# The residual x as transposes at the head of the output projection's accumulation group, in place of identity products at its end

## The chip, the cores and the metric

The kernel runs on one core of one Trainium2 chip. The metric is the device time of one execution, in microseconds (us). The kernel before was timed in three runs, and the median counts. Beside them stands one profiled execution, from which all durations and starts of single instructions come; it is its own execution, with its own time.

## What is computed

The input x has 256 channels and 48 x 48 positions, that is 2304 tokens of 256 numbers, all in float32. Two layers follow each other. Cut to what matters, with `gn` a normalization over groups of channels and `ln` one over each token:

```
# layer 0
xt  = tokens of gn(x)                       # 2304 x 256
q, k, v = xt @ Wq.T + bq, xt @ Wk.T + bk, xt @ Wv.T + bv
A   = softmax(q @ k.T / 8)                  # every token's 4 heads are rows of their own: 9216 x 9216, head size 64
t   = x.T + (A @ v) @ Wo.T + bo             # the residual x is added, as tokens
# layer 1
t   = t + slice_attention(ln(t))            # 64 soft slices, attention among them, back to tokens
t   = t + moe(ln(t))                        # 8 experts, each token in its two best
out = t.T as 256 x 48 x 48
```

The change lies in the line that makes t in layer 0. The kernel holds x with its channels on the partitions, while t has its tokens on the partitions, so x has to be turned where it is added.

## The kernel before, in words

The work has stages, one after the other: projections of q, k and v (to about 69 us of the profiled execution's span), attention (to about 1244 us), the slice attention of layer 1, the routing of tokens to experts, the experts, and a last transposition of the output.

Attention takes the 9216 queries in 18 blocks of 512 (`NQB`), and for every block all 9216 keys in 36 pairs of 128-key tiles (`NPAIR`). For a pair, `scores` (line 507) makes four score products on TensorE (PE) into PSUM tile `s`, and ScalarE (ACT) takes their exponential into `p`. `sums` adds `p` into `acc` on VectorE (DVE), and `times_values` (line 539) makes the four value products into PSUM tile `av`. The value products of a pair come on PE after the score products of the next. All these products use a 64 x 64 part of PE's array each. A float32 product is two passes on PE, and each pass leaves its own record in the profile with its own weight load (PEld). So a pair has eight records of `s` and eight of `av`.

After a block comes `close` (line 552), in which DVE makes `both` from `acc` and `up` from `av`. Then comes `between` (line 584), called at the second pair of the next block. It calls `follow` (line 572), which puts up to four steps of a side pipeline on PE, each for another 128-token tile:

- `out_proj` (line 373) for tile k-2: the attention output `OT` of that tile times `WoT`, with two channel halves c that add up, and then the tile's columns of `x_sb` times the identity matrix `ident`, one product for each 128 channels, each into its own half of the 256 columns. All of it is one accumulation group in the first 256 columns of PSUM tile `pa`. In each of these calls the first operand is the stationary one, whose load is the weight load; in the profile's names the moving operand comes first (`pa<-ident,x_sb`).
- `turn` (line 407) for the tile before that: two transposes of the normalized tile `tn`, into the other columns of `pa`.
- `slices` (line 417): the slice logits, into `pb`.
- `gather` (line 453): sums of tokens by slice, into `pb`.

`between` then adds the softmax sums `pb<-both,ones` to PE's stream. What these steps need of DVE and ACT (in `out_proj`: `add`, which reads `pa` and adds the bias `bo_bc` into `t_sb`, then `spread` and `norm`) is put into a list in the order of a rank written beside each step, and one entry is taken from that list at each of the following pairs.

`out_proj` is called for tiles 0 to 15 inside attention and for tiles 16 and 17 after it, in the loop at line 666, where the PSUM tile is called `pm`. There all of the last block's outputs have to be finished first.

The order on every engine is written out by hand: `pe`, `dve`, `act` and `pool` are wrapped in `InOrder` (line 49), which keeps instructions in program order. Line 57, where the wrapper issues, therefore stands for most instructions in the profile, and one goes by the tiles' names. Semaphore waits are put in by the tile framework from the tiles' uses.

Of the kernel before, what the change touches and what calls it, by code (L numbers as in the profile page):

```python
# [15 lines left out]
P = 128  # L16
# [46 lines left out]
def layers(  # L63
# [14 lines left out]
    pe, dve, act, pool = (InOrder(tc, e) for e in (nc.tensor, nc.vector, nc.scalar, nc.gpsimd))  # L78
# [73 lines left out]
    x_sb = l0.tile([P, 2, NT], FP, name="x_sb")  # L152
# [77 lines left out]
    with proj, tc.tile_pool(name="ps_pj", bufs=5, space=PSUM) as ps_pj, tc.tile_pool(  # L230
# [80 lines left out]
        for i in range(NTT):  # L311
            pv = ps_pj.tile([P, 512], FP, name="pp", tag="pp")
            for c in range(2):
                nc.tensor.matmul(  # L314
                    pv[:, 0:C], xn[:, c, i * P : (i + 1) * P], WvT[:, c, :],
                    start=(c == 0), stop=(c == 1),
# [11 lines left out]
        for ci in range(2):  # L328
            cols = slice(ci * P, (ci + 1) * P)
            for k in range(2):  # L330
                nc.tensor.matmul(
                    pw[:, ci * S : (ci + 1) * S], W0T[:, k, cols], Ws_sb[:, k, :],
                    start=(k == 0), stop=(k == 1),
                )
            for k in range(2):
                nc.tensor.matmul(
                    pw[:, 192 + ci * E : 192 + (ci + 1) * E], WoutT[:, k, cols], Wg_sb[:, k, :],
                    start=(k == 0), stop=(k == 1),
# [34 lines left out]
    def out_proj(i, ps):  # L373

        tok = slice(i * P, (i + 1) * P)
        g, u = divmod(i, TG // P)
        for c in range(2):
            pe.matmul(
                ps[:, 0:C], OT[:, g % 2, c, u * P : (u + 1) * P], WoT[:, c, :],
                start=(c == 0), stop=False,  # L380
            )
        for c in range(2):
            pe.matmul(
                ps[:, c * P : (c + 1) * P], x_sb[:, c, tok], ident, start=False, stop=(c == 1)
            )

        def add():
            dve.tensor_tensor(t_sb[:, i, 0:C], ps[:, 0:C], bo_bc, ALU.add)

        def spread():  # L390
            s6 = small.tile([P, 6], FP, name="s6", tag="s6")
            dve.bn_stats(s6, t_sb[:, i, 0:C])
            dve.bn_aggr(stats[:, i, :], s6)
            ve = small.tile([P, 1], FP, name="ve", tag="ve")
            dve.tensor_scalar(ve, stats[:, i, 1:2], 1e-5, None, ALU.add)
            pool.tensor_tensor(rstd_t[:, i : i + 1], ve, mhalf[:, 0:1], ALU.pow)
            return ve

        def norm():
            dve.tensor_scalar(  # L400
                tn[:, i % 6, :], t_sb[:, i, 0:C], stats[:, i, 0:1], rstd_t[:, i : i + 1],
                ALU.subtract, ALU.mult,
            )

        return [(2, add), (3, spread), (7, norm)]
# [67 lines left out]
    def attention():  # L473


        with tc.tile_pool(name="pexp", bufs=5) as pexp, tc.tile_pool(
# [95 lines left out]
            def follow(k):  # L572

                pa = ps_side.tile([P, 512], FP, name="pa", tag="pa")
                pb = ps_side.tile([P, 512], FP, name="pb", tag="pb")
                work = []
                for lag, (step, ps) in enumerate(
                    ((out_proj, pa), (turn, pa), (slices, pb), (gather, pb))
                ):
                    if 0 <= k - 2 - lag < NTT - 2:  # L580
                        work.extend(step(k - 2 - lag, ps))
                return work, pb
# [83 lines left out]
    for k, step in enumerate((out_proj, turn, slices)):  # L666
        work = []
        for i in range(NTT - 2, NTT):
            work.extend(step(i, ps_o.tile([P, 512], FP, name="pm", tag="pm")))
        if k == 0:  # L670
            weights_transposed(0, 4)
            weights_transposed(4, 4)
        if k == 2:
            pe.matmul(den, ones, sw_sum, start=True, stop=False)
        for w in in_turn(work):
            w()
    for c in range(2):
        for i in range(NTT - 2, NTT):
            pe.matmul(
                pts[:, c * S : (c + 1) * S], tn[:, i % 6, c * P : (c + 1) * P], sw[:, i, :],  # L680
                start=(i == NTT - 2), stop=(i == NTT - 1),
# [19 lines left out]
    with tc.tile_pool(name="sa", bufs=1) as sa:  # L701
        tw = sa.tile([P, C + E], FP, name="tw")
        with sums_done, tc.tile_pool(name="ps_b", bufs=4, space=PSUM) as ps_b, tc.tile_pool(
# [4 lines left out]
            for m in range(2):  # L708
                for c in range(2):
                    pe.matmul(  # L710
                        ph[:, m, :], W0_sb[:, c, m * P : (m + 1) * P], ts_sum[:, c * S : (c + 1) * S],
                        start=(c == 0), stop=(c == 1),
# [23 lines left out]
            for u in range(2):  # L736
                ph = ps_b.tile([P, 2, S], FP, name="ph", tag="mm")
                phs.append(ph)
                for kind in range(2):
                    j = 2 * kind + u  # L740
                    for c in range(2):
                        pe.matmul(
                            ph[:, kind, :], Wqkv_sb[:, c, j * P : (j + 1) * P], hsT[:, c, :],
                            start=(c == 0), stop=(c == 1),
# [62 lines left out]
            for w in range(2):  # L807
                pe.matmul(
                    pw, tokT[:, w].rearrange("p a s -> p (a s)"), Wout_sb[:, w, :],
                    start=(w == 0), stop=(w == 1),  # L810
# [407 lines left out]
```

## Time and profile before

| What | Value |
|---|---|
| Median of three timed runs | 1645.1 us (1644.57 to 1647.49) |
| Profiled execution's own time | 1642.84 us |
| Span of the profiled execution, first to last instruction | 1641.1 us |
| Mean granted PE clock | 0.973 of full |
| PE busy, 69 to 1238 us (attention) | 1167.46 of 1169.00 us |
| DVE and ACT busy there | 899.75 and 683.15 us |
| `pa<-WoT,OT`, 128x256, records in attention | 64, mean 405 ns |
| `pa<-ident,x_sb`, 128x128, records in attention | 64, mean 274 ns |
| `pm<-ident,x_sb`, 128x128, records after attention | 8, mean 375 ns |

How to read it: a PE record lasts from the start of a pass to its result's arrival, and the next pass starts long before that. So records overlap, and the sum of their durations is more than the time that they take from PE. The time that a pass takes is the distance from its start to the next one's. In a timeline, the first number is the start in us from the span's start, the second how long the whole group of records lasted, and brackets hold the idle time of that engine before it with what ended it.

### The profile page before, as it was taken

What the parts mean: (1) busy time and instruction counts of PE and PEld (TensorE: products, weight loads), DVE (VectorE), ACT (ScalarE), POOL (GpSimd) and SP (SyncE); (2) the same over time, 40 slices, a digit from 0 to 9 for tenths busy, and PEclk for the clock granted to TensorE, in tenths of its full rate; (3) what the DMA queues carried; (4) which work ended last, traced back from release to release, by engine and by line L of the source; (5) the groups of instructions that cost most, each with busy time, mean ns of one, the idle gap of its engine ahead of it and who ended that gap; (6) DMA issues with size and microseconds to landing.
All of it is one profiled execution on the core that took longest, in us unless ns stands there. A gap on an engine that the chain in (4) does not pass through costs nothing.

```text
span 1641.1 us, 31749 instructions
## 1 busy us (share of the span) xinstructions
PE 1574.2 (96%) x13178; PEld 793.9 (48%) x13178; DVE 1046.9 (64%) x1361; ACT 811.1 (49%) x1100; POOL 149.7 (9%) x129
## 2 busy tenths in 40 slices
PE   7999999999999999999999999999997589999995
PEld 3633343333333333333333333333344389999994
DVE  6577777687787786877777878878785721111111
ACT  2355555565555655656556556556552313333321
POOL 0000000000000000000000000000000253333321
PEclk9999999999999999999999999999997679999998
DMA  4000000000000000000000000000005456666665
GB/s 135 1 1 1 1 1 1 1 1 1 2 1 1 2 1 2 1 1 1 1 1 1 1 1 1 1 1 1 1 2 185 161 174 186 172 188 183 176 164 169
DMA packets 39878, 79.26 MB, mean 48 GB/s; under 512 B 3581, under 2 KB 26186, under 8 KB 39594
## 3 DMA queue, kind: packets, MB, share of 16 engines
q1 hardware_dynamic: 32042, 66.35, 12.1%
q0 software_dynamic: 7680, 10.75, 3.7%
q8 instruction: 108, 1.77, 0.5%
q14 instruction: 48, 0.39, 0.1%
HBM read 64.64 MB, written 12.45 MB: 47 GB/s over the span
## 4 chain that ended last, share of the span: by engine, by line
PE 93%; DVE 3%; DMA 3%; ACT 0%; issue 0%; POOL 0%; SPq 0%; ACTq 0%; POOLq 0%; DVEq 0%
PE s L57 34%; PE av L57 34%; PE ph L57 8%; PE py L57 8%; PE pa L57 2%; DMA t_d<-y,slot_t 2%; PE pb L57 1%; PE pw L57 1%; PE pp L285 1%; PE pp L289 1%; PE pp L314 1%; PE pt L57 1%; DVE s L57 0%; DMA Wq_raw<-in_L_conv_Wq_dram 0%; PE pm L57 0%; ACT p L57 0%
## 5 line engine op out<-in xcount | busy, mean ns | idle before, releaser
L57 DVE TENSOR_TENSOR acc<-acc,p 128x1024 f32<-128x1024 f32 x612 | 748.1, 1222 | 256.7 <-ACT p L57 248.8
L57 ACT ACTIVATE p<-s 128x1024 f32<-128x1024 f32 x648 | 663.3, 1024 | 492.9 <-PE s L57 482.8
L57 PE MATMUL av<-p,v_sb 64*64 64x512 f32 x5184 | 675.8, 590 | 1.4 <-ACT p L57 0.7
L57 PE MATMUL s<-q,kk 64*64 64x512 f32 x5184 | 674.9, 589 | 0.0
L57 PEld LDWEIGHTS s<-q,kk 64*64 64x64 f32 x5184 | 202.0, 133 | 351.2 <-issue 180.9
L57 PEld LDWEIGHTS av<-p,v_sb 64*64 64x64 f32 x5184 | 195.8, 131 | 358.1 <-ACT p L57 202.3
L57 ACT ACTIVATE hid<-ph,bcol 128x128 f32<-128x128 f32 x312 | 89.4, 368 | 221.3 <-PE ph L57 220.6
L57 PEld LDWEIGHTS ph<-xT,w 128*128 128x128 f32 x1248 | 147.7, 195 | 2.8 <-DVE xT L57 0.9
L57 PE MATMUL ph<-xT,w 128*128 128x128 f32 x1248 | 148.1, 278 | 0.5 <-DVE xT L57 0.5
L57 PE MATMUL py<-w_sb,hid 128*128 x624 | 147.1, 379 | 0.0
L57 POOL TENSOR_TENSOR rstd_t<-ve,mhalf 128x1 f32<-128x1 f32 (+1 forms) x21 | 27.5, 1312 | 1252.1 <-DVE ve L57 1252.1
L57 DVE COPY xT<-pt 128x256 f32<-128x256 f32 x40 | 17.0, 425 | 172.6 <-PE pt L57 172.6
L57 PEld LDWEIGHTS py<-w_sb,hid 128*128 128x128 f32 x624 | 112.8, 190 | 12.2
L1086 POOL DMA_INDIRECT t_d<-y,slot_t x39 | 61.7, 1583 | 98.7 <-DVE y L57 88.4
L57 DVE TENSOR_TENSOR y<-py,b_bc 128x256 f32<-128x256 f32 x39 | 16.6, 425 | 68.6 <-PE py L57 68.6
L1026 POOL DMA_INDIRECT xs<-tn_d,slot_t x36 | 38.3, 1064 | 93.0 <-PE pt L57 83.9
L57 DVE RECIPROCAL rinv<-pb 128x256 f32<-128x256 f32 x18 | 31.5, 1750 | 0.0
L57 DVE TENSOR_TENSOR acc<-p 128x1024 f32<-128x1024 f32 x18 | 22.1, 1225 | 8.4 <-ACT p L57 8.4
L302 DVE TENSOR_SCALAR q<-pp,bcol 64x512 f32<-64x512 f32 (+1 forms) x30 | 20.8, 694 | 9.4 <-PE pp L285 9.1
L57 PE MATMUL pw<-what,t_sb 128*128 128x86 f32 x72 | 15.7, 422 | 6.7 <-POOL what L57 6.7
L57 DVE TENSOR_REDUCE up<-av 128x512 f32<-128x1024 f32 x18 | 21.9, 1216 | 0.0
L285 PE MATMUL pp<-t_sb,WqT 128*128 128x512 f32 (+1 forms) x40 | 19.0, 601 | 0.3 <-DVE t_sb L276 0.3
(251 smaller groups left out, 607.5 us busy)
## 6 DMA issues: line engine op xcount, KB each, us to landing
w<-in_L_ffn_W_dram SPq DMA_DIRECT2D x40, 1024.0 KB, 5.3
w_sb<-in_L_ffn_W_dram SPq DMA_DIRECT2D x8, 1024.0 KB, 10.6
x_sb<-in_x_dram SPq DMA_DIRECT2D x4, 576.0 KB
t_d<-t_sb SPq DMA_DIRECT2D x3, 768.0 KB, 3.9
tn_d<-tn SPq DMA_DIRECT2D x3, 768.0 KB, 3.7
tt<-t_d SPq DMA_DIRECT2D x4, 512.0 KB
out_dram<-ob SPq DMA_DIRECT2D x4, 512.0 KB, 3.5
b_bc<-in_L_ffn_b_dram SPq DMA_DIRECT2D x1, 1024.0 KB
```

What stands on the lines that cost most here:

```text
L57: return self.tc.keep_in_program_order(getattr(self.engine, name)(*args, **kwargs))
L285: nc.tensor.matmul(pq[:, 0:tn], WqT[:, c, cols], xn[:, c, toks], start=(c == 0), stop=(c == 1))
L289: nc.tensor.matmul(pk[:, 0:tn], WkT[:, c, cols], xn[:, c, toks], start=(c == 0), stop=(c == 1))
L302: nc.vector.tensor_scalar(dst, pq[rows, 0:tn], bcol[rows, B_Q + m : B_Q + m + 1], 0.125, ALU.add, ALU.mult,)
L314: nc.tensor.matmul(pv[:, 0:C], xn[:, c, i * P : (i + 1) * P], WvT[:, c, :], start=(c == 0), stop=(c == 1),)
L1026: nc.gpsimd.indirect_dma_start(out=xs, out_offset=None, in_=tn_d[:, :], in_offset=bass.IndirectOffsetOnAxis(ap=slot_t[:, s : s + 1], axis= ...
L1086: nc.gpsimd.indirect_dma_start(out=t_d[:, :], out_offset=bass.IndirectOffsetOnAxis(ap=slot_t[:, s : s + 1], axis=0), in_=y, in_offset=None ...
```

## The change

In `out_proj`, x comes first. Its two products become transposes (the flag `is_transpose`, with the same operands), the first of which opens the accumulation group. The two projection products follow, add onto what the transposes wrote, and close the group. Nothing else is edited; the function serves both places that call it.

```diff
         g, u = divmod(i, TG // P)
+
+        for c in range(2):
+            pe.matmul(
+                ps[:, c * P : (c + 1) * P], x_sb[:, c, tok], ident, start=(c == 0), stop=False,
+                is_transpose=True,
+            )
         for c in range(2):
             pe.matmul(
                 ps[:, 0:C], OT[:, g % 2, c, u * P : (u + 1) * P], WoT[:, c, :],
-                start=(c == 0), stop=False,
-            )
-        for c in range(2):
-            pe.matmul(
-                ps[:, c * P : (c + 1) * P], x_sb[:, c, tok], ident, start=False, stop=(c == 1)
+                start=False, stop=(c == 1),
             )
```

More of the change, by code (lines that the diff above doesn't have):

```diff
@@ L378, in out_proj @@
             pe.matmul(
-                ps[:, 0:C], OT[:, g % 2, c, u * P : (u + 1) * P], WoT[:, c, :],
-                start=(c == 0), stop=False,
+                ps[:, c * P : (c + 1) * P], x_sb[:, c, tok], ident, start=(c == 0), stop=False,
+                is_transpose=True,
             )
@@ L383, in out_proj @@
             pe.matmul(
-                ps[:, c * P : (c + 1) * P], x_sb[:, c, tok], ident, start=False, stop=(c == 1)
+                ps[:, 0:C], OT[:, g % 2, c, u * P : (u + 1) * P], WoT[:, c, :],
+                start=False, stop=(c == 1),
             )
```

## Prediction

> **What bounds the kernel now.** I read the page first: busy shares, then the chain that ended last.
>
> ```profile
> PE 1574.2 (96%) x13178; PEld 793.9 (48%) x13178; DVE 1046.9 (64%) x1361; ACT 811.1 (49%) x1100; POOL 149.7 (9%) x129
> ...
> PE 93%; DVE 3%; DMA 3%; ACT 0%; issue 0%; POOL 0%; SPq 0%; ACTq 0%; POOLq 0%; DVEq 0%
> ```
>
> TensorE (PE) holds 93% of the chain, so a piece taken from its stream shortens the span unless something else arrives late in its place. Next the groups of tile pa, the PSUM bank in which `out_proj` works.
>
> ```profile
> L57 PE MATMUL pa<-WoT,OT x64: 379/379/483, 259.2 to 1197.5; 128*128 128x256 f32 x64
> ...
> L57 PE MATMUL pa<-ident,x_sb x64: 272/275/275, 260.1 to 1198.0; 128*128 128x128 f32 x64
> ...
> L57 PE MATMUL pa<-ident,tn x32: 272/273/328, 324.6 to 1213.3; 128*128 128x128 f32 x32
> ```
>
> Attention treats 16 tiles, so the 32 identity products of x left 64 records, two passes each; the 32 transposes of tn, same shape and type, left 32, one pass each. The durations (275 and 273 ns) are alike and say nothing of the price, because records overlap. The price is the distance between starts, and the timeline of PE has it. Here is one boundary between query blocks, with ScalarE (ACT) and VectorE (DVE) just after it:
>
> ```profile
> 712.76 1.13 PE L57 MATMUL pa<-WoT,OT 128*128 128x256 f32 x4
> 713.08 0.81 PE L57 MATMUL pa<-WoT,OT 128*128 128x256 f32 x3
> 713.73 0.61 PE L57 MATMUL pa<-ident,x_sb 128*128 128x128 f32 x4
> 714.17 0.38 PE L57 MATMUL pa<-ident,tn 128*128 128x128 f32 x2
> 714.39 0.56 PE L57 MATMUL pb<-Wl,tnT 128*128 128x72 f32 x4
> ...
> 717.98 1.02 ACT L57 ACTIVATE p<-s 128x1024 f32<-128x1024 f32 x1 [3.42 <-PE s L57]
> 719.04 1.23 DVE L57 TENSOR_TENSOR acc<-acc,p 128x1024 f32<-128x1024 f32 x1 [3.86 <-ACT p L57]
> ```
>
> (The second line is the same group from its second pass on.) Second to fourth projection pass: 0.65 us, 0.216 each. Four x passes: 0.44, 0.11 each. Two tn transposes: 0.22, again 0.11 each. The first projection pass takes 0.32, since its weight load lies open. At the block's other end ACT and DVE stand idle for 3.42 and 3.86 us, waiting for PE.
>
> The last block has one place where one-pass transposes come first after attention's narrow products, and the end of attention has tiles 16 and 17:
>
> ```profile
> 1213.16 0.44 PE L57 MATMUL pa<-ident,tn 128*128 128x128 f32 x2
> 1213.44 0.23 PE L57 MATMUL pb<-Wl,tnT 128*128 128x72 f32 x1
> ...
> 1244.71 2.05 PE L57 MATMUL pm<-WoT,OT 128*128 128x256 f32 x4 [4.33 <-DVE ends_of L57]
> 1246.55 1.06 PE L57 MATMUL pm<-ident,x_sb 128*128 128x128 f32 x4
> 1247.40 1.91 PE L57 MATMUL pm<-WoT,OT 128*128 128x256 f32 x4
> 1247.65 0.42 DVE L57 TENSOR_TENSOR t_sb<-pm,bo_bc 128x256 f32<-128x256 f32 x1 [3.08 <-PE pm L57]
> 1249.11 0.78 PE L57 MATMUL pm<-ident,x_sb 128*128 128x128 f32 x4
> 1249.93 0.42 DVE L57 TENSOR_TENSOR t_sb<-pm,bo_bc 128x256 f32<-128x256 f32 x1 [1.85 <-PE pm L57]
> ```
>
> Two transposes at the head take 0.28, open load included. At the end PE starts cold after a wait of 4.33 us for DVE (mean granted clock 0.57 from 1242 to 1250 us), so passes take twice as long: 1.71 for four of projection, 0.85 for four of x. The second add on DVE, at 1249.93, starts all that follows.
>
> **What the Trainium skill says.** "Perfetto Trace Analysis", section Transposes, advises the transpose mode for logical transposes, since it skips the arithmetic. The trace agrees in passes: 32 records against 64. "TensorE: Matmul & The Clock Gate", Part 4, gives about 275 ns for a transpose inside a kernel. The record agrees (273), but the pitch that matters here is 110. The same page, Part 2, LDWEIGHTS, prices a load by its columns, 128/1.2 = 107 ns; that fits 110, so a one-pass transpose is load-bound and no cheaper than one x pass. "PSUM — Partial Sum Buffer", The four PSUM rules, says that an fp32 transpose sets the written bits and that a later product without the opening flag adds onto them. It gives no cost, and no line of this trace shows a product adding onto a transpose.
>
> **The change part by part.**
>
> *Passes removed.* Each tile's x goes from four passes to two.
>
> *Order.* Transposes now open the group and projection closes it. Old stage, 712.76 to 714.17: 1.41 us. New stage: 0.28 for two transposes at the head (from 1213.16 to 1213.44) plus 4 x 0.216 = 0.86 of projection, whose loads hide under the pass before: 1.14. That is 0.27 less per tile: two passes, 0.22, and 0.05 from an open load under which the second transpose's own load begins sooner. Low end 0.22, if the 0.05 isn't had. 16 x 0.27 = 4.3 us, low end 3.5.
>
> *Waits.* The built instruction order shows the wait on DVE for the free bank moved from the first projection pass to the first transpose; attention's next products and the softmax sums `pb<-both` are queued behind it, but it was met long before, since the records show no idle PE there. The sums also need both, which DVE has at 258.86 in the tightest block, 1.80 before they start at 260.66. The next block's `av` needs DVE's up: in that block up ends at 259.99 and `av` starts at 261.24, a cover of 1.25 of which 0.27 goes. If it were gone, `av` would wait and the gain with it.
>
> *What is late next.* DVE works without a gap for some 13 us after 719, which could take a gain back. But that stretch begins after 3.86 us idle, released by ACT, and ACT by PE, so it moves forward with PE. DVE's add of this tile comes 12 us later (726.41); who reads PSUM doesn't matter. No DMA, SP or POOL instruction is moved.
>
> *Tiles 16 and 17.* Their first transpose carries the same waits on DVE and PE in the built order, so it can't use the 4.33 us. From PE's start to the second add: now 5.22. After, at the cold clock: 0.54 for two transposes at the head (the 0.28 about doubled), 1.71, 0.43 (half of 0.85), 1.71, and 0.25 until the add (1247.40 to 1247.65): 4.64. Saved 0.6; between 0.4 and 0.9, as the clock comes back earlier or later. The path goes on through this add, so it passes on whole.
>
> *After a transpose.* The unseen step is projection adding onto a fresh transpose. From below: nothing, as passes of x that add onto projection follow at 0.11. From above: PE waits for the transpose to drain, 0.273 in place of 0.11, so 0.16 a tile, 2.9 in 18. A gain is excluded, since the pass's load and stream remain. I take nothing.
>
> *Sum.* 4.3 + 0.6 = 4.9 us. On the profiled execution: span 1641.1 to 1636.2, its time 1642.84 to 1637.9. That execution lies 2.3 below the median of the three timed runs, so I take the saving from the median: 1645.1 - 4.9 = 1640.2. Ends without a stall: 3.5 + 0.4 and 4.4 + 0.9, so 1641.2 to 1639.8.
>
> **Rivals.**
>
> 1. *A drain after each transpose pair.* 18 x 0.16 = 2.9 given back: 1643.1, within 0.2%. For it: it is the one step that the trace lacks. Against: tn transposes are followed by other products at 0.11, and x's second pass adds onto its first at the same pitch.
>
> 2. *Slower: the clock.* Part 4 of the TensorE page says that transposes don't count as PE work for the clock. If two more of them at each boundary emptied one activity window (the page's Part 1: about 3.4 us), half a clock there would cost an estimated 1.7 us. In each of 16 boundaries that is 27: 1645.1 - 4.9 + 27 = 1667. It cancels the gain from three such windows on, and makes the kernel slower by over 0.2% from five. Against: tn's transposes are there already, and the granted clock is 1.00 over 21 to 1242 us.
>
> 3. *Not one pass.* If x still took two passes, only the reordering's 0.05 a tile would stay: 0.9 in 18, 1644.2. The tn records speak against it.
>
> 4. *Clock draws after attention.* The clock's mean is 0.62 from 1250 to 1331 us, and the three runs spread over 2.9 us. A draw 1.7 worse leaves 3.2 of the gain: 1641.9.
>
> **How the numbers follow.** Forecast 0.72; rival 1, 0.08; rival 2, 0.04; rival 3, 0.03; rival 4, 0.13. 0.2% is 3.3 us, about what a measurement of this kernel can tell from no change. The forecast lies 1.6 beyond it, inside the runs' spread: I give 0.66 of its chance and 0.08 of rival 4's to faster, and what is left, with rivals 1 and 3, to the same: 0.74, 0.21, 0.05 (rival 2 and 0.01 of scatter). The range runs from 1637.5, the low end 1639.8 less the 2.3 by which the profiled execution undercut the median, to 1643.3, which takes in rivals 1 and 4.
>
> **What would show it.** In the profile after: `pa<-ident,x_sb` x32 in place of x64; from the first transpose to the start of the tn group 1.14 us, with the first projection pass 0.11 behind the second transpose (0.27 would be rival 1); from one block's first `pa` product to the next block's 64.84 us (now 65.11, from 777.87 to 842.98); from PE's start to the second add after attention about 4.6; clock 1.00 all through attention (rival 2 if not). I would be wrong if the blocks shorten and the stretch after attention grows as much.

## The result, and the profile after

| | before | after |
|---|---|---|
| Median | 1644.84 us (6 runs, 1642.54 to 1647.49) | 1639.88 us (6 runs, 1638.26 to 1640.73) |
| Profiled execution, its own time | 1642.84 us | 1639.97 us |
| Its span | 1641.1 us | 1638.2 us |
| Its mean granted PE clock | 0.973 | 0.972 |

After to before is 0.9968, with a 95% interval of 0.9955 to 0.9981: 5.0 us less by the medians, 3.1 to 7.4 by the interval. The forecast was 4.9 less, 1640.2. The two spans differ by only 2.9; where the other 2 us lie is told below. First the page after: the line of busy time and the shares of the chain.

```profile
PE 1571.7 (96%) x13142; PEld 789.9 (48%) x13142; DVE 1046.7 (64%) x1361; ACT 810.3 (49%) x1100; POOL 149.8 (9%) x129
...
PE 93%; DVE 3%; DMA 3%; ACT 0%; issue 0%; POOL 0%; SPq 0%; ACTq 0%; POOLq 0%; DVEq 0%
```

PE still holds 93% of the chain and has 36 records less, which is two for each of 18 tiles. The groups of tile pa after the change (shortest, median and longest duration in ns):

```profile
L57 PE MATMUL pa<-WoT,OT x64: 379/379/382, 259.1 to 1193.2; 128*128 128x256 f32 x64
...
L57 PEld LDWEIGHTS pa<-ident,x_sb x32: 137/140/143, 258.8 to 1192.3; 128*128 128x128 f32 x32
L57 PE MATMUL pa<-ident,x_sb x32: 272/300/329, 258.8 to 1192.4; 128*128 128x128 f32 x32
```

x has 32 records in place of 64. Their median duration went up, from 275 to 300 ns, while the stage got shorter: once more the duration isn't the price. Their weight loads (PEld) have 140 ns; the identity products' had 190, same shape and type. The boundary of the same block as before the change, on the timeline of PE, and ACT and DVE just after it:

```profile
710.50 0.44 PE L57 MATMUL pa<-ident,x_sb 128*128 128x128 f32 x2
710.77 1.03 PE L57 MATMUL pa<-WoT,OT 128*128 128x256 f32 x4
711.64 0.38 PE L57 MATMUL pa<-ident,tn 128*128 128x128 f32 x2
711.86 0.56 PE L57 MATMUL pb<-Wl,tnT 128*128 128x72 f32 x4
...
715.45 1.02 ACT L57 ACTIVATE p<-s 128x1024 f32<-128x1024 f32 x1 [3.15 <-PE s L57]
716.50 1.23 DVE L57 TENSOR_TENSOR acc<-acc,p 128x1024 f32<-128x1024 f32 x1 [3.58 <-ACT p L57]
```

From the first transpose to the tn group 711.64 - 710.50 = 1.14 us, where it was 1.41. The idle times of ACT and DVE shrink by the same 0.27 (3.42 to 3.15, 3.86 to 3.58), so both move forward with PE and neither becomes late. The end of attention, PE and DVE:

```profile
1240.01 0.66 PE L57 MATMUL pm<-ident,x_sb 128*128 128x128 f32 x2 [4.33 <-DVE ends_of L57]
1240.46 1.91 PE L57 MATMUL pm<-WoT,OT 128*128 128x256 f32 x4
1242.17 0.63 PE L57 MATMUL pm<-ident,x_sb 128*128 128x128 f32 x2
1242.60 1.91 PE L57 MATMUL pm<-WoT,OT 128*128 128x256 f32 x4
...
1244.55 0.42 DVE L57 TENSOR_TENSOR t_sb<-pm,bo_bc 128x256 f32<-128x256 f32 x1 [1.71 <-PE pm L57]
```

From PE's start to the second add 4.54 us; it was 5.22.

**Where the time went, by stages.** To compare profiles I cut each at instructions that all of them have: the first score product, the end of the last division (OT), the start of the second of the two adds above, the first expert product (`ph<-xT,w`), and the first expert product of the third slot (a slot holds 128 token places for one expert). All in us, from the starts and ends in the trace; the fourth column is the sum of the two before it.

| profile | attention | OT to add | add to experts | OT to experts | first two expert slots |
|---|---|---|---|---|---|
| before | 1174.70 | 6.29 | 79.79 | 86.08 | 13.55 |
| before, again (e7) | 1174.71 | 6.18 | 79.75 | 85.93 | 18.14 |
| before, third (e8) | 1174.70 | 5.49 | 79.78 | 85.27 | 17.71 |
| after | 1170.37 | 5.61 | 80.39 | 86.00 | 15.80 |
| after, again (e5) | 1170.38 | 5.41 | 80.57 | 85.98 | 17.67 |
| after, third (e9) | 1170.38 | 5.60 | 80.62 | 86.22 | 17.71 |

Attention is 4.33 shorter in each pair, 16 x 0.27. The two adds come 0.45 earlier on the mean, but the experts don't start earlier after it: 85.76 before, 86.07 after. And the first two expert slots scatter by 4.6 us for a reason of their own. They took 2.25 us more in the first profile after than in the first one before, and that is why the two spans differ by less than the medians.

### The profile page after: what moved, and what is told of

Its sections match the earlier page's. It is cut to its first block, busy times and chain, and to the rows that moved or that the text cites. A ratio compares the mean times of both kernels' runs of the same rounds, so it can differ in the third digit from the quotient of the medians.

```text
span 1638.2 us, 31677 instructions
## 1 busy us (share of the span) xinstructions
PE 1571.7 (96%) x13142; PEld 789.9 (48%) x13142; DVE 1046.7 (64%) x1361; ACT 810.3 (49%) x1100; POOL 149.8 (9%) x129
## 4 chain that ended last, share of the span: by engine, by line
PE 93%; DVE 3%; DMA 3%; ACT 0%; issue 0%; POOL 0%; SPq 0%; ACTq 0%; POOLq 0%; DVEq 0%
PE s L57 34%; PE av L57 34%; PE ph L57 9%; PE py L57 8%; DMA t_d<-y,slot_t 2%; PE pa L57 1%; PE pb L57 1%; PE pw L57 1%; PE pp L285 1%; PE pp L289 1%; PE pp L314 1%; PE pt L57 1%; DVE s L57 0%; DMA Wq_raw<-in_L_conv_Wq_dram 0%; PE pm L57 0%
```

## The experiments

**Is the transpose cheap, or its place?** The first four kernels ran on one chip, timed against the same runs of before (1641.47 us). e1 keeps the order of the kernel before, with the projection first, and makes x's products one-pass transposes there. Against the kernel before:

```diff
         for c in range(2):
             pe.matmul(
-                ps[:, c * P : (c + 1) * P], x_sb[:, c, tok], ident, start=False, stop=(c == 1)
+                ps[:, c * P : (c + 1) * P], x_sb[:, c, tok], ident, start=False, stop=(c == 1),
+                is_transpose=True,
             )
```

> The projection opens the group as before, and x follows as two one-pass transposes that add onto it and close it: the pass count alone, without the new order. Theory (two passes of 0.11 us less, and 0.05 more only because a transpose stands at the head): from the first projection pass to the start of the tn transposes 1.19 us (1.41 before, 1.14 with the transposes first), so 0.22 a tile in attention; 4.0 us in all against the kernel before, a ratio near 0.9976. Rival (the order brings the gain, the passes don't): 1.41 and no difference. Rival (a transpose that adds onto a product drains the array): over 1.3.

Measured: 1637.1 us, ratio 0.9977 (0.9969 to 0.9985); attention 3.61 shorter than before. Timeline of PE, same block:

```profile
710.07 1.13 PE L57 MATMUL pa<-WoT,OT 128*128 128x256 f32 x4
711.04 0.38 PE L57 MATMUL pa<-ident,x_sb 128*128 128x128 f32 x2
711.25 0.38 PE L57 MATMUL pa<-ident,tn 128*128 128x128 f32 x2
```

The stage is 1.18 (711.25 - 710.07), where it was 1.41, and the two transposes take 0.21 where four passes took 0.44. So 0.23 of the 0.27 a tile is the pass count alone, without the new order.

e2 does the other part alone: x first, projection last, without the flag `is_transpose`, so in two passes. Against the change:

```diff
                 ps[:, c * P : (c + 1) * P], x_sb[:, c, tok], ident, start=(c == 0), stop=False,
-                is_transpose=True,
             )
```

> x comes first, as two-pass identity products that open the group, and the projection closes it: the order alone. Theory of the prediction's rival sum: 0.05 a tile, the stage 1.36 us, 0.8 us in all. A second theory, from the records after the change: the 0.05 is had because a transpose's own weight load is shorter when it lies open (the second load starts 0.06 after the first transpose and 0.11 after a two-pass product); then the stage stays at 1.41 and the time doesn't move (ratio 0.999 to 1.001).

Measured: 1640.61 us, ratio 0.9999 (0.9991 to 1.0007); attention 0.05 longer. Timeline of PE:

```profile
711.28 0.71 PE L57 MATMUL pa<-ident,x_sb 128*128 128x128 f32 x4
711.83 1.03 PE L57 MATMUL pa<-WoT,OT 128*128 128x256 f32 x4
712.69 0.38 PE L57 MATMUL pa<-ident,tn 128*128 128x128 f32 x2
```

and, from the groups of tile pa in e2, the weight loads:

```profile
L57 PEld LDWEIGHTS pa<-ident,x_sb x64: 186/190/192, 257.6 to 1195.6; 128*128 128x128 f32 x64
```

1.41 again: the order alone is worth nothing. The first four passes take 0.55 at the head, 0.11 more than behind other work, just the open load that the projection no longer shows (its first pass took 0.32 and now 0.22). What the full change has beyond the pass count goes with the transpose's own load, whose record lasts 140 ns in place of 190. By the single records of the full change, the second transpose's load starts 0.06 us after the first transpose, and the second transpose 0.17 after it; in e2 the next load starts 0.11 after the first pass, and the next pass 0.21.

**Does a product pay for adding onto a fresh transpose?** In e4 the transposes write columns of their own and the projection opens its own group. x is left out of t here, so the routing differs and the time isn't read; the stage is. Against the change:

```diff
-                ps[:, c * P : (c + 1) * P], x_sb[:, c, tok], ident, start=(c == 0), stop=False,
+                ps[:, C + c * P : C + (c + 1) * P], x_sb[:, c, tok], ident, start=(c == 0), stop=(c == 1),
...
-                start=False, stop=(c == 1),
+                start=(c == 0), stop=(c == 1),
```

> The transposes write into the other 256 columns of the same PSUM tile, which nobody adds onto, and the projection opens a group of its own: x is left out of t (so the routing of tokens differs, and only the stage in attention is to be read, not the whole time). Theory (adding onto a fresh transpose costs nothing): from the first transpose to the tn group 1.14 us, as with the change. Rival (part of the stage after the change is a wait for the transposes' results): shorter than 1.14.

```profile
709.09 0.44 PE L57 MATMUL pa<-ident,x_sb 128*128 128x128 f32 x2
709.36 1.03 PE L57 MATMUL pa<-WoT,OT 128*128 128x256 f32 x4
710.23 0.38 PE L57 MATMUL pa<-ident,tn 128*128 128x128 f32 x2
```

1.14 us, as with the change. Adding onto a transpose costs nothing.

**Do more transposes disturb the clock?** e3 makes the two transposes twice (the second pair opens the group anew). Against the change:

```diff
         for c in range(2):
             pe.matmul(
+                ps[:, c * P : (c + 1) * P], x_sb[:, c, tok], ident, start=(c == 0), stop=(c == 1),
+                is_transpose=True,
+            )
+        for c in range(2):
+            pe.matmul(
```

> Each tile's two transposes are made twice, the second pair opening the group anew, so that the output stays as it is: four transposes ahead of the projection. Theory (0.11 us a transpose, wherever it stands): the stage 1.36 us, 0.22 a tile more than with the change as it is, 3.5 in attention and 0.4 to 0.9 after it, so about 1 us faster than the kernel before, and within 0.2% of it. Rival (transposes let the clock fall, since they don't count as work): with four in place of two the granted clock in attention falls below 1.00 and the time rises by 1.7 us for each window lost.

Measured: 1641.14 us, ratio 1.0000 (0.9992 to 1.0009). The boundary on the timeline of PE:

```profile
711.47 0.66 PE L57 MATMUL pa<-ident,x_sb 128*128 128x128 f32 x4
711.96 1.03 PE L57 MATMUL pa<-WoT,OT 128*128 128x256 f32 x4
712.83 0.38 PE L57 MATMUL pa<-ident,tn 128*128 128x128 f32 x2
```

and attention in the windows view of e3 (stretch, length, then busy time and count of PE, PEld, DVE, ACT and POOL, the granted clock, DMA share, GB/s):

```profile
21.00:1240.00 1219.00, 1215.18 (x10912) 469.70 (x10910) 932.39 (x1053) 697.27 (x737) 22.32 (x16) 1.00 0.01 2
```

Two more transposes add 0.22 to the stage (1.36), 0.11 each, and attention is still 0.85 shorter than before (1173.85). The clock stays 1.00 through attention with up to six transposes at a boundary, some 0.65 us in 65. So few can't show whether a transpose counts as work for the clock.

**Does the tail pass its gain on?** e5 is the change itself once more, on the chip on which e6 to e9 ran too (before there: 1645.09 us).

> The changed kernel once more, unedited, for a second profile of it and as the measure for the next kernel. In its first profile the first two expert slots took 9.03 and 6.76 us (7.60 and 5.95 before), 2.2 us more. Theory (that was this one execution, since the change touches nothing there): about 7.5 and 5.95, and a ratio to the kernel before of 0.9965 to 0.9975. Rival (the earlier start of the experts runs into the weights' transfers): again about 9 us.

Measured: 1640.25 us, ratio 0.9966 (0.9954 to 0.9978). Its tail has 5.41 to the add, but the experts start no earlier (table above). Its first expert slots took 9.99 and 7.68 us, where 7.5 was expected for the first. e7 and e8 are the kernel before, e9 the change again, to see whose that is.

> The kernel before, unedited, for its profile on the chip of the next three runs. In its first profile the first two expert slots took 7.60 and 5.95 us; with the change they took 9.03 and 6.76, then 9.99 and 7.68, with several engines standing still at once and nothing in the profile that released them. Theory (such a standstill comes and goes from execution to execution and has nothing to do with the change): in some profile of the kernel before the first slot is over 9 us too. Rival (the earlier start brings it): in both profiles of the kernel before about 7.6.

> The kernel before once more, as the run ahead of it: the same theories and numbers.

> The changed kernel on the same chip. Theory (comes and goes): first expert slot like that of the kernel before on this chip, between 7.4 and 10 us. Rival (the earlier start brings it): over 9 us here and 7.6 for the kernel before. By either, the stage in attention is 1.14 us and the blocks 64.84.

Single times 1646.82, 1644.76 and 1641.33 us. The first two expert slots in e7, the kernel before, on the timeline:

```profile
1337.74 1.14 ACT L57 ACTIVATE hid<-ph,bcol 128x128 f32<-128x128 f32 x4 [3.57 <-remote]
1339.17 0.42 DVE L57 COPY xT<-pt 128x256 f32<-128x256 f32 x1 [10.03 <-remote]
```

and in the first profile after:

```profile
1333.45 1.14 ACT L57 ACTIVATE hid<-ph,bcol 128x128 f32<-128x128 f32 x4 [3.55 <-remote]
1333.49 0.42 DVE L57 COPY xT<-pt 128x256 f32<-128x256 f32 x1 [8.61 <-remote]
```

ACT and DVE wait there for something that the profile calls remote and doesn't name. Before and after have it alike (the slots take 18.14, 17.71 and 17.71 us in e7, e8 and e9), so it isn't the change's. It goes with the chip: all five profiles on this one, e5 to e9, have 17.62 to 18.14, while e1 to e4 and e10 to e12, on two other chips, have 13.22 to 13.56. That is also about the difference between the times of the kernel before on these chips (1645.09 against 1641.47 and 1641.15). What the releaser is stays open.

Then each part of the change alone, and a test of the clock, on another chip (before there: 1641.15 us). e10 has the transposes for tiles 16 and 17 only, e11 for tiles 0 to 15 only; `residual` and `projection` hold the two loops of `out_proj` (not shown):

```diff
+        if i >= NTT - 2:
+            residual(True, is_transpose=True)
+            projection(False)
+        else:
+            projection(True)
+            residual(False)
```

(e11: `i < NTT - 2`.)

> One part alone: attention's 16 tiles as before the change (projection opens, two-pass identity products close), and only tiles 16 and 17 after attention open with one-pass transposes. Prediction's theory (the tail's 0.6 passes on whole): from the end of the last division to the first expert product 85.2 us, against 85.8 in three profiles of the kernel before, and the ratio 0.9996. Rival theory (the clock takes it back: after a shorter run of tail products only one activity window is granted at full clock instead of two): the division to the second add takes about 5.5 us in place of 6.0, but the add to the first expert product 80.5 in place of 79.8, together 86.0 or so, ratio 1.000. Attention as before in both: 1174.7 us.

> The other part alone: transposes open the group in attention's 16 tiles, and tiles 16 and 17 stay as before the change. Both theories: attention 1170.4 us, 4.3 less than before. Prediction's theory: the stretch from the last division to the first expert product is 85.8, as before, so this kernel is 0.6 us slower than the full change. Rival theory: the same 85.3 to 86.1 as either kernel, ratio to before 0.9974, no slower than the full change.

Measured: e10 1640.54 us, ratio 0.9997 (0.9988 to 1.0005); e11 1637.44 us, ratio 0.9979 (0.9972 to 0.9987). Attention 1174.70 in e10 and 1170.35 in e11, as expected. OT to experts 5.32 + 80.05 = 85.37 in e10, and 6.35 + 79.81 = 86.16 in e11. So e10, against the rival's 86.0, is near the 85.2 of passing on: 0.8 below e11, 0.4 below the mean of the three profiles of before. e1, whose tail has one-pass transposes too, agrees with 5.34 + 79.93 = 85.27. But single profiles scatter as widely: e8, the kernel before, has 85.27 as well. What sets e10 apart from the change shows in the windows view for the 6.8 us from the second add on. The change, first profile after:

```profile
1244.55:1251.35 6.80, 4.02 (x22) 3.21 (x20) 4.46 (x21) 2.70 (x8) 1.18 (x2) 0.75 0.76 255
```

e10, the tail only:

```profile
1248.16:1254.96 6.80, 3.12 (x23) 2.37 (x21) 4.83 (x23) 2.70 (x8) 1.19 (x2) 0.97 0.76 264
```

The granted clock is 0.75 against 0.97. With finer stretches, full clock lasts from 1245.25 to 1248.66 in the change's profile, 3.4 us, and from 1247.7 to 1254.5 in e10, 6.8: one window of 3.4 us against two. The Trainium skill, "TensorE: Matmul & The Clock Gate", Part 1, says that the clock is judged over free-running windows of about 3.4 us, so that the same kernel meets them in another phase each time; the stretches of 3.4 and 6.8 agree. All three profiles of the change had a mean clock of 0.72 to 0.75 there, and 80.4 to 80.6 from the add to the experts, and so had e4, with transposes at the head too (0.73 and 80.6). e1, e3 and e10 (transposes in the tail too), e2, e11 and the three of before had 0.91 to 0.97, and 79.4 to 80.1. So the shorter tail doesn't lose the second window in itself: after the division, e10's PE stream is that of the change. The traces show one difference, in where the windows fall. The first stretch of full clock begins 4.78 and 4.85 us after OT in e1 and e10, and 5.04 to 6.31 after it in the three profiles of the change and e4. That is a hint that with the shorter tail the second window hangs on how much of the tail still falls into the first; no run moved the windows to test it.

e12 keeps PE busy through the wait of 4.33 us: the full change, and nine products whose result nobody reads, put behind attention's last product into a tile that is free (`behind["pa"]`; how it is handed on is not shown).

```diff
             extremes()
+            for n in range(9):
+                pe.matmul(
+                    behind["pa"][:, 0:C], x_sb[:, 0, 0:P], WoT[:, 0, :], start=(n == 0), stop=(n == 8)
+                )
```

> The full change, and nine two-pass products of 256 columns into a free tile put behind attention's last product, to fill most of the 4.33 us in which TensorE waits for VectorE; their result is read by nobody. If the clock is what eats the tail's gain, tiles 16 and 17 now run at full clock: from TensorE's first transpose to the second add 2.5 us in place of 4.5, the granted clock 1.00 from 1234 to about 1243, and the stretch from the last division to the first expert product falls to some 83 to 84.5 from 86.1; ratio to before about 0.9955. If the clock has nothing to do with it, the first figure stays at 4.5 and the stretch at 86.

Measured: 1633.98 us, ratio 0.9956 (0.9942 to 0.9969). Timeline of PE and DVE:

```profile
1235.06 4.15 PE L57 MATMUL pa<-WoT,x_sb 128*128 128x256 f32 x18
1239.46 0.41 PE L57 MATMUL pm<-ident,x_sb 128*128 128x128 f32 x2 [0.24 <-DVE ends_of L57]
1239.70 1.03 PE L57 MATMUL pm<-WoT,OT 128*128 128x256 f32 x4
...
1241.85 0.42 DVE L57 TENSOR_TENSOR t_sb<-pm,bo_bc 128x256 f32<-128x256 f32 x1 [0.66 <-PE pm L57]
```

and the tail in the windows view of e12:

```profile
1234.00:1247.50 13.50, 10.13 (x56) 7.89 (x56) 9.48 (x25) 3.28 (x9) 1.18 (x2) 1.00 0.33 96
```

PE's idle falls from 4.33 to 0.24 us, the clock is 1.00 over the whole stretch (0.75 over the same stretch of the change's profile), and from the first transpose to the second add it takes 2.39 us in place of 4.54. The tail doesn't begin earlier: its first transpose starts 1.07 us after OT in both. OT to experts: 3.46 + 79.81 = 83.27, against 86.07 with the change. So the clock sets the price of the tail, and this saving passes on.

e6 shortens the tail in another way: the transposes of tiles 16 and 17 are made before attention's last wait, into that free tile, so that only the projection waits for OT.

```diff
+    def residual(i, ps, opens=True):
+        ...
+                if b == NQB - 1:
+                    for n in range(2):
+                        residual(NTT - 2 + n, pa[:, n * C : (n + 1) * C], opens=(n == 0))
+                    st["pa"] = pa
...
+            for n in range(2):
+                work.extend(
+                    out_proj(
+                        NTT - 2 + n, behind["pa"][:, n * C : (n + 1) * C], turned=True,
+                        closes=(n == 1),
+                    )
+                )
```

> With the change, and the transposes of tiles 16 and 17 made ahead of attention's last wait, in the tile pa that the last block leaves unused, so that only projections are left after it, and those wait for the attention output alone and no more for the PSUM bank. Theory (a transpose needs nothing but x, so it can fill PE's idle time): from the end of the last division on DVE to the second add about 3.0 us (5.61 with the change: 1.07 until PE starts and 4.54), so 2.6 us faster than the change, a ratio near 0.9955 to the kernel before. Rival (the path after attention ends elsewhere, so that an earlier add is lost again): no more than 0.5 us below the change.

Measured: 1638.93 us, ratio 0.9954 (0.9940 to 0.9967). OT to the add 3.36, but add to experts 81.08, together 84.44: 1.6 less than the change's 86.07, where the add alone came 2.2 earlier. The granted clock is 0.50 through the 6.8 us after the add, without any stretch of full clock, so part of the gain is lost as with the change. Against the change's own 1640.25 on this chip it is 1.3 less by the medians, with intervals that overlap: the saving shows in the stage, and not surely in the time.

## Why the prediction came out right, and where its steps failed

- **Pass count.** Right: x32 in place of x64, and e1 gives it 0.23 a tile without any change of order.
- **0.27 a tile, 4.3 in attention.** Right in size: 1.14 us, 64.84 forecast between blocks and 64.83 measured (775.34 to 840.17), 4.33 in each pair of profiles.
- **The 0.05 from an open load.** The size held, the reason by half. It named the second transpose's load, and that load does start sooner; but it booked the sum under order, and rival 3 gave the reordering alone 0.05 a tile, 0.9 in all. e2 shows nothing for it. The 0.05 needs both, a transpose and the head of the group: e1, with transposes at the end, has 3.61 in attention where the change has 4.33, so 0.045 less a tile.
- **"A one-pass transpose is load-bound".** Open. It came from the skill's load price of 107 ns ("TensorE: Matmul & The Clock Gate", Part 2, LDWEIGHTS) and a pitch of 110. At the head of the group the single records fit it: at 710.50 the second transpose starts 0.17 after the first and 0.11 after its own load, and in e2 a pass starts 0.21 after the first and again 0.11 after its load. Behind other work they can't tell, since half of the 0.216 of a pass of 256 columns is 0.11 too. No run with fewer columns was made. The forecast didn't rest on it, as the price came from the tn group.
- **Waits, and what is late next.** Right: idle times shrink by 0.27 on both engines, and no new wait appears.
- **Drain (rival 1), clock in attention (rival 2), two passes (rival 3).** e4, e3 and the record count put each aside.
- **Clock draws after attention (rival 4).** Right in kind: from the add to the experts the change took 80.53 on the mean against 79.77 before, 0.75 for the lost window, where the rival priced a worse draw at 1.7.
- **Tiles 16 and 17, 0.6.** PE's start to the second add: 4.64 forecast, 4.54 measured (the two transposes at the cold head took 0.45, not 0.54), so the first half held. The step that failed is "so it passes on whole". In three profiles of the change the time from OT to the experts is 86.07 on the mean against 85.76 before; the products after the add met one window of full clock where they had met two. e10 had two, and there 0.4 to 0.8 passed on, by what it is held against, which one profile doesn't prove. By time, the tail alone is worth 0.5 less by ratio, with an interval from 2.0 less to 0.8 more: it can't be told from nothing. e12 shows the clock to be the lever. So the tail counts for zero to 0.8 here, as the windows fall.
- **Sum.** 4.9 forecast, 5.0 by medians, of which 4.33 is shown stage by stage. The remaining 0.6 is as large as the tail's forecast, but the medians don't prove it: their interval is 4 us wide, and the expert slots alone scatter by more. The stages of the three profiles give attention's 4.33 and nothing from the tail, so that the forecast met the medians to 0.3 us is luck in its last part.

Of the versions that keep the whole computation, e12 has the lowest time: 1633.98 us. On its chip that is 3.5 less than e11 (1633.26 to 1635.24 against 1635.90 to 1640.16), whose tail is that of before. Against the change the stage says 2.8 less; the ratios (0.9956 and 0.9968, from different chips) have intervals that overlap.

## What to carry to other kernels

Turning a float32 tile by a product with the identity cost two passes here, by a transpose one; price it by the distance between starts, for the records' durations went the other way. A saving on the engine that the chain of waits names passed on whole in attention, where the clock was 1.00 throughout. After a wait of 4.33 us it didn't pass on in three profiles, because the clock that followed differed. There, filling the wait with products that nobody reads was worth more than the two saved passes of each tile (2.8 against at most 0.8 us in that stage).

## What the runs showed of the hardware that was not expected

- A transpose's weight load has a shorter record than that of a float32 product of the same shape: 140 against 190 ns.
- A transpose may open an accumulation group or close one: the pitch beside it stays 0.11 for 128 columns and 0.216 for 256 either way (the change, e1).
- The same tail of the same kernel takes 5.49 or 6.29 us to the second add, by where the clock's windows of 3.4 us fall: in e8 half clock lasts 3.4 us and ends 1.3 us before that add, in the first profile of the kernel before it lasts 6.8 us and ends 0.5 us before it.
- The first two expert slots take 13.55 to 18.14 us in one and the same kernel (before), with several engines held at once by a releaser that the profile doesn't name. The long ones, 17.62 and more, are all of one chip.
